# Two convolution blocks on one core: the 7x7 convolution's transfers split by partition halves between two queues, and the group norms' sums read out of their bank at once

## The chip, the cores and the metric

The kernel runs on one core of one Trainium2 chip. The metric is the device time of one execution in microseconds (us). A core has TensorE (PE in the profile, with PEld for the loading of its weights), VectorE (DVE), ScalarE (ACT), GpSimd (POOL) and SyncE (SP). Transfers are carried by 16 DMA engines. In this kernel SP and POOL each issue transfers on a queue of their own (q1 and q0 in the profile); ACT issues a few.

## The reference

The input x is (8, 96, 96, 192) in float32. Two blocks follow one another, each added to its input:

```python
# layer 0
x = x + L0(_gn(x))   # 192 -> 384 projection, 3x3 depthwise conv, four decaying scans,
                     # layer norm over channels, 384 -> 192 projection
# layer 1
x = x + L1(_gn(x))   # 7x7 depthwise conv, layer norm, 192 -> 768, gelu, 768 -> 192, scale

def _gn(v, G=32, eps=1e-5):
    g = v.reshape(B_, H_, W_, G, C_ // G)
    m = jnp.mean(g, axis=(1, 2, 4), keepdims=True)
    s = jnp.var(g, axis=(1, 2, 4), keepdims=True)
    return ((g - m) / jnp.sqrt(s + eps)).reshape(v.shape)
```

`_gn` is a group norm: the mean and the variance of 32 groups of 6 channels, for each of the 8 images. The 7x7 convolution works on every channel by itself.

## The kernel before

Five stages follow one another. The order of instructions on each engine is written out by hand (`tc.manual_schedule`): every engine works off its own list in program order.

- **A** (about 47 to 783 us of the span): for each image, 12 units. A unit turns a piece of the image with transposes (`turn`, L351, evicted with the group norm's scale and shift by ACT at L358 or DVE at L356), multiplies it by `win` (`project_full` L365, `project_rest` L378) and stores it. The transposes use a pool `pt` of two PSUM banks. While image b is projected, the statistics of image b+1 are gathered (`bn_stats` L320), and in units 9 to 11 the steps of its group norm are placed among the projection (`ends`, L468): `means` in unit 9, `squares` in 10, `powers` and `shift` later in 10, the spreading in 11.
- **B** (783 to 1846 us): the 3x3 convolution, as products with a band matrix, and the scans.
- **C** (1846 to 2930 us): 96 units of four blocks (`block_c`, transposes L833 and products L835), each finished one unit later by `finish_c` on DVE (`x1u`, L858, which empties the PSUM banks `po`, and `x1c`, L871). The group norm of the next layer, for a pair of images at a time, is gathered at L887, and its steps come one to a unit, each placed behind the unit's products and ahead of `finish_c`. It has a PSUM bank of its own (`gn_ps`).
- **D** (2930 to 3510 us): the 7x7 convolution. 16 steps of 12 channels (`conv_d`, L1030); the 12 are two sets of 6, called m = 2i and 2i+1. `load_d(m)` brings one set: six `xin` transfers (L753) and two `band` transfers (L758), of 64 partitions each; SP loads partitions 0 to 63 and GpSimd 64 to 127. Five sets fit, so set m waits until the convolution has done with set m-5. `scale_d` (DVE, L1015) applies the group norm to a set, one step ahead of its use. ACT evicts a step's outputs to `yo` (L1041; two buffers), with the first set's outputs in partitions 0 to 63 (k = 0) and the second set's in 64 to 127 (k = 1), and `store_d` (L1070) stores them to `Y_d`, all on GpSimd, k by turns. In the last step the first quarter of each row goes by SP (L1069) and the rest by GpSimd.
- **E** (3510 us to the end): the layer norm and the two big products. Its first load `y` (L1122) is on SP and reads the first quarter of the rows of `Y_d`.

The group norm's own steps are in `norm_steps` (L32). `means` sums the per-chunk means on DVE (L49), and two products with `avg` (L51, L52) put the group means into a PSUM bank; `squares` copies these out (`gm` L57, `mean` L59), sums the squares (L61 to L69) and multiplies them by `avg` (L71) into a second bank; `powers` reads that (`ve`, L75) and takes the power -0.5 on GpSimd; `shift` follows. Then `spread` brings scale and shift to all partitions (L332 in A; L903 and L911 in C).

In the profile the digits of a name are dropped: `X1_d`, `Y_d` and `Z2_d` stand there as `X_d`, `Y_d` and `Z_d`.

Of the kernel before, what the change touches and what calls it, by code (L numbers as in the profile page):

```python
# [8 lines left out]
F32 = mybir.dt.float32  # L9
AF = mybir.ActivationFunctionType  # L10
ALU = mybir.AluOpType
AX = mybir.AxisListType
# [3 lines left out]
GROUPS = 32  # L16
GN_EPS = 1e-5
# [14 lines left out]
def norm_steps(nc, pool, psum, tag, st, avg, count, neg_half):  # L32

    rows, n, k, _ = st.shape
    sub = 2 * k
    sv = st.rearrange("p n k (e t) -> p n (k e) t", t=3)  # L40
    rb = pool.tile([n, 2], F32, tag="gn_rb", name="gn_rb")
    t = {}

    def bank():
        return psum.tile([128, 512], F32, tag=tag, name="gn_ps")

    def means():
        ms = pool.tile([rows, n], F32, tag="gn_ms", name="gn_ms")
        nc.vector.tensor_reduce(ms, sv[:, :, :, 1], AX.X, ALU.add)  # L49
        t["ps"] = ps = bank()  # L50
        nc.tensor.matmul(ps[:, :n], avg, ms, start=True, stop=True)  # L51
        nc.tensor.matmul(ps[:n, n : n + 1], ms, avg[:, 0:1], start=True, stop=True)  # L52

    def squares():

        gm = pool.tile([rows, n], F32, tag="gn_gm", name="gn_gm")
        nc.vector.tensor_scalar(gm, t["ps"][:rows, :n], 1.0 / sub, None, ALU.mult)  # L57
        t["mean"] = mean = pool.tile([n, 1], F32, tag="gn_mean", name="gn_mean")
        nc.vector.tensor_scalar(mean, t["ps"][:n, n : n + 1], -1.0 / sub, None, ALU.mult)  # L59
        d = pool.tile([rows, n, sub], F32, tag="gn_d", name="gn_d", bufs=1)  # L60
        nc.vector.tensor_tensor(  # L61
            d, sv[:, :, :, 1], gm.unsqueeze(2).to_broadcast([rows, n, sub]), ALU.subtract
        )
        nc.vector.tensor_tensor(d, d, d, ALU.mult)
        nc.vector.scalar_tensor_tensor(
            d, sv[:, :, :, 2], 1.0 / count, d, ALU.mult, ALU.add
        )
        ds = pool.tile([rows, n], F32, tag="gn_ds", name="gn_ds")
        nc.vector.tensor_reduce(ds, d, AX.X, ALU.add)  # L69
        t["ps"] = ps = bank()  # L70
        nc.tensor.matmul(ps[:n, 0:1], ds, avg[:, 0:1], start=True, stop=True)  # L71
# [12 lines left out]
@with_exitstack  # L84
def conv_blocks_kernel(
# [31 lines left out]
    nc = tc.nc  # L117
    B, S, _, D = x.shape
# [8 lines left out]
    GS = D // GROUPS  # L127

    const = ctx.enter_context(tc.tile_pool(name="const", bufs=1))
# [9 lines left out]
    BP = B // 2  # L139
    PH = 3  # L140
# [18 lines left out]
    HB = 21  # L159
# [12 lines left out]
    ones = const.tile([64, 128], F32, name="ones")  # L172
    nc.vector.memset(ones, 1.0)


# [47 lines left out]
    with ExitStack() as ph:  # L223
# [14 lines left out]
            nc.scalar.dma_start(bin_, b_in.rearrange("(m p) -> p m", p=128))  # L238


        member = cp.tile([GROUPS, 2, GROUPS, GS], F32, name="member")
        for i in range(2):
            nc.vector.tensor_copy(
                member[:, i],
                ident[:GROUPS, :GROUPS].unsqueeze(2).to_broadcast([GROUPS, GROUPS, GS]),
            )
        memberf = member.rearrange("p i g s -> p (i g s)")

# [222 lines left out]
        with tc.manual_schedule():  # L471
# [13 lines left out]
            for b in range(B):  # L485
                more = b + 1 < B
                for t in range(n_t):
# [28 lines left out]
                    k, j = divmod(t, NJ)  # L516
# [250 lines left out]
    with ExitStack() as ph:  # L767
# [108 lines left out]
        def group_steps(x1c, k, i):  # L876


            bp, part = divmod(k, NH)
            n = part * NS + i  # L880
            if n == 0:
                gn[0] = sp.tile([S, 2 * GROUPS, NH * NS, 6], F32, tag="gn_st", name="gn_st", bufs=1)
            st = gn[0]
            w = slice(i * WC // NS, (i + 1) * WC // NS)

            def step(b, g):
                nc.vector.bn_stats(  # L887
                    st[:, b * GROUPS + g, n], x1c[:, g * GS : (g + 1) * GS, w, b]
                )

            bn = [lambda b=b, g=g: step(b, g) for g in range(GROUPS) for b in range(2)]
            per = -(-len(bn) // (n_s - 1))
            steps = [bn[j : j + per] for j in range(0, len(bn), per)]
            if n < NH * NS - 1:
                return steps
            last, rb = norm_steps(nc, sp, ps_s, "gn_ps", st, avg, GS * WC // NS // 2, neg_half)
            held = []

            def spread():

                dg = sp.tile([2 * GROUPS, 2, 2 * GROUPS], F32, tag="gn_dg", name="gn_dg", bufs=1)
                for a in range(2):
                    nc.vector.tensor_scalar(  # L903
                        dg[:, a],
                        ident[: 2 * GROUPS, : 2 * GROUPS],
                        rb[:, a : a + 1],
                        None,
                        ALU.mult,
                    )
                ps = ps_s.tile([128, 512], F32, tag="gn_ps", name="ps_s1")  # L910
                nc.tensor.matmul(  # L911
                    ps[:, : 4 * GROUPS],
                    ones[: 2 * GROUPS],
                    dg.rearrange("p a g -> p (a g)"),
                    start=True,
                    stop=True,
                )
# [79 lines left out]
    with ExitStack() as ph:  # L997
# [12 lines left out]
        def scale_d(m, xin):  # L1010
            xv = xin.rearrange("q t a c (v b) -> q t a c v b", b=2)
            for b in range(B):
                sc, sh = (s1[:, a, b % 2, b // 2, m : m + 1] for a in range(2))
                xw = xv[:, :, b // 2, :, :, b % 2]
                nc.vector.tensor_scalar(xw, xw, sc, sh, ALU.mult, ALU.add)  # L1015
# [30 lines left out]
                        scale=1.0,  # L1046
                    )

        def store_d(yo, i):
            for bl in range(NB):  # L1050

                pieces = [(3, HB - 3)]
                if bl == 0:
                    pieces.append((HB - 3, HB))
                if bl == NB - 1:
                    pieces.append((0, 3))
                for k in range(2):
                    c = i * CD + k * HC
                    for lo, hi in pieces:
                        r = (S - HB - bl * HG) * PH  # L1060
                        src = yo[k * 64 + lo * PH : k * 64 + hi * PH, bl]
                        dst = Y_d[r + lo * PH : r + hi * PH, c // HC].rearrange(
                            "r b a c n -> r (b a c n)"
                        )
                        src = src.rearrange("r a c n -> r (a c n)")

                        n = NV * HC * 2 * WQ if i == D // CD - 1 else 0
                        if n:
                            nc.sync.dma_start(dst[:, :n], src[:, :n])  # L1069
                        nc.gpsimd.dma_start(dst[:, n:], src[:, n:])  # L1070
# [265 lines left out]
```

## Time and profile before

| | |
|---|---|
| median of 10 runs | 5964.9 us (5962.51 to 5969.27) |
| the profiled execution | 5969.09 us |
| its span, first to last instruction | 5967.3 us |
| mean granted TensorE clock | 0.974 |
| busy: PE, PEld, DVE, ACT, POOL | 95%, 66%, 58%, 41%, 44% of the span |
| q0 (GpSimd), q1 (SP) | 450.64 MB in 24.0%, 593.38 MB in 38.5% of the 16 engines' span |

A line of the timeline has the start in us, the time it took in us, the engine, the line of the kernel and the operation, what it writes and reads, how many instructions are merged, and in brackets how long the engine had been idle before and what released it. "SPq" and "POOLq" are the issuing side of a queue. A line of a windows table has the window, its length, the busy time and number of instructions of PE, PEld, DVE, ACT and POOL, the granted clock, the mean busy share of the 16 DMA engines, and GB/s. A line of the DMA view by queue has the packets, the MB and the time they took as a share of the window.

### The profile page before, as it was taken

What the parts mean: (1) busy time and instruction counts of PE and PEld (TensorE: products, weight loads), DVE (VectorE), ACT (ScalarE), POOL (GpSimd) and SP (SyncE); (2) the same over time, 40 slices, a digit from 0 to 9 for tenths busy, and PEclk for the clock granted to TensorE, in tenths of its full rate; (3) what the DMA queues carried; (4) which work ended last, traced back from release to release, by engine and by line L of the source; (5) the groups of instructions that cost most, each with busy time, mean ns of one, the idle gap of its engine ahead of it and who ended that gap; (6) DMA issues with size and microseconds to landing.
All of it is one profiled execution on the core that took longest, in us unless ns stands there. A gap on an engine that the chain in (4) does not pass through costs nothing.

```text
span 5967.3 us, 122712 instructions
## 1 busy us (share of the span) xinstructions
PE 5647.7 (95%) x48550; PEld 3956.8 (66%) x48550; DVE 3452.5 (58%) x8023; ACT 2429.5 (41%) x6146; POOL 2613.4 (44%) x2835
## 2 busy tenths in 40 slices
PE   6999989999998999999687769999999999999999
PEld 3655633333336989898666647777777777777777
DVE  5555469999995667777623234444444444444443
ACT  2444457777775555555343322222222222222222
POOL 1111148888886666666433323333333333333332
PEclk9999989999999999999888879999999999999999
DMA  7999779999987888888899953232323232323221
GB/s 203 284 282 262 219 208 245 246 244 244 244 236 202 263 262 265 263 267 261 240 292 289 289 154 79 64 80 64 80 62 77 64 80 63 79 64 80 64 64 39
DMA packets 634143, 1054.48 MB, mean 177 GB/s; under 512 B 108976, under 2 KB 508929, under 8 KB 633569
## 3 DMA queue, kind: packets, MB, share of 16 engines
q1 hardware_dynamic: 510192, 593.38, 38.5%
q0 software_dynamic: 117248, 450.64, 24.0%
q8 instruction: 384, 6.29, 0.5%
q10 hardware_dynamic: 6128, 2.61, 0.2%
q14 instruction: 191, 1.56, 0.1%
HBM read 585.19 MB, written 476.72 MB: 178 GB/s over the span
## 4 chain that ended last, share of the span: by engine, by line
PE 78%; DMA 6%; DVE 1%; issue 1%; POOL 1%; SPq 0%; ACT 0%; POOLq 0%; DVEq 0%; ACTq 0%
PE po L1225 19%; PE po L835 14%; PE hp L1195 12%; PE pl L582 10%; PE hp L1205 7%; PE pa L603 5%; PE pt L833 4%; PE py L1030 3%; DMA Y_d<-yo 3%; PE pa L606 2%; DMA xin<-X_d 2%; PE pt L1178 2%; DVE xin L1015 1%; DMA X_d<-x1c 0%; SPq L1069 0%
## 5 line engine op out<-in xcount | busy, mean ns | idle before, releaser
L1214 ACT ACTIVATE g<-hp,b0g 128x384 f32<-128x384 f32 x1152 | 563.3, 587 | 1834.5 <-PE hp L1205 1834.5
L1225 PE MATMUL po<-w1g,g 128*128 128x192 f32 x6912 | 1162.7, 327 | 0.0
L1225 PEld LDWEIGHTS po<-w1g,g 128*128 128x128 f32 x6912 | 1121.7, 190 | 1.1 <-issue 1.1
L835 PE MATMUL po<-wc,mt 128*96 128x193 f32 x4608 | 913.0, 333 | 0.0
L1182 DVE COPY yT<-pt 128x384 f32<-128x384 f32 x288 | 248.5, 863 | 1044.0 <-PE pt L1178 1043.6
L1195 PE MATMUL hp<-yT,w0w 128*128 128x384 f32 x2304 | 782.4, 490 | 0.4 <-DVE yT L1182 0.4
L835 PEld LDWEIGHTS po<-wc,mt 128*96 128x96 f32 x4608 | 701.8, 163 | 68.6 <-ACT mean L839 65.1
L1243 POOL DMA_DIRECT2D out_dram<-xo x576 | 340.3, 593 | 880.8 <-DVE xo L1232 847.3
L582 PE MATMUL pl<-pin,band 34*32 34x380 f32 (+1 forms) x13824 | 629.1, 489 | 18.6 <-DMA pin<-P_d 18.6
L1195 PEld LDWEIGHTS hp<-yT,w0w 128*128 128x128 f32 x2304 | 429.8, 191 | 257.9 <-issue 4.3
L612 DVE TENSOR_TENSOR_SCAN z<-decay,loc 128x768 f32<-128x768 f32 x288 | 505.9, 1756 | 59.6 <-ACT loc L591 30.3
L652 POOL TENSOR_TENSOR mo<-mo,z 128x768 f32<-128x768 f32 x288 | 529.4, 1839 | 3.4 <-ACT mo L607 0.4
L1030 PE MATMUL py<-xin,band 63*64 63x248 f32 (+1 forms) x6912 | 400.4, 391 | 133.7 <-DVE xin L1015 133.7
L29 POOL TENSOR_TENSOR rs<-rs_ve,neg_half 96x8 f32<-96x8 f32 x96 | 159.1, 1657 | 830.1 <-DVE rs_ve L28 830.1
L621 DVE TENSOR_TENSOR_SCAN z<-decay,z 128x768 f32<-128x768 f32 x288 | 498.2, 1730 | 0.0
L582 PEld LDWEIGHTS pl<-pin,band 34*32 34x32 f32 x13824 | 232.9, 107 | 396.9 <-issue 395.7
L1030 PEld LDWEIGHTS py<-xin,band 63*64 63x64 f32 x6912 | 334.4, 141 | 199.3 <-DVE xin L1015 125.3
L842 ACT ACTIVATE sq<-pt,mean 96x384 f32<-96x384 f32 x768 | 442.9, 577 | 25.7 <-ACT mean L839 0.8
L603 PE MATMUL pa<-loc,mix 128*32 128x384 f32 x3456 | 431.9, 493 | 0.0
L606 PE MATMUL pa<-last,down 96*32 96x384 f32 x1152 | 426.8, 493 | 0.9 <-ACT mo L607 0.9
L1205 PE MATMUL hp<-yT,w0w 64*128 64x384 f32 x2304 | 423.5, 500 | 0.0
L365 PE MATMUL pm<-xT,win 128*128 128x384 f32 x1152 | 397.3, 495 | 5.0 <-DVE po L389 5.0
(116 smaller groups left out, 7682.9 us busy)
## 6 DMA issues: line engine op xcount, KB each, us to landing
P_d<-po POOLq DMA_DIRECT2D x96, 1152.0 KB, 9.7
pin<-P_d SPq DMA_DIRECT2D x192, 576.0 KB
mt<-M_d SPq DMA_DIRECT2D x576, 192.0 KB
xq<-in_x_dram SPq DMA_DIRECT2D x96, 576.0 KB
xr<-in_x_dram SPq DMA_DIRECT2D x384, 144.0 KB
X_d<-x1u POOLq DMA_DIRECT2D x192, 288.0 KB, 4.1
X_d<-x1c SPq DMA_DIRECT2D x192, 288.0 KB
y<-Y_d SPq DMA_DIRECT2D x24, 2304.0 KB
```

What stands on the lines that cost most here:

```text
L582: nc.tensor.matmul(pls[g][at * RB : (at + 1) * RB, :, lo:hi], band[rows, c, kh, :], pin[rows, c, :, NJ - 1 - j, lo + kh - 1 : hi + kh - 1] ...
L603: nc.tensor.matmul(pa[at], mix[:, i, at], loc[:, q], start=True, stop=True)
L606: nc.tensor.matmul(pa[at], down[:, to], last[:, q], start=True, stop=True)
L612: nc.vector.tensor_tensor_scan(zf, decay_f, loc.rearrange("p q n -> p (q n)"), 0.0, ALU.mult, ALU.add)
L621: nc.vector.tensor_tensor_scan(zr, decay_f, zr, 0.0, ALU.mult, ALU.add)
L652: nc.gpsimd.tensor_tensor(m, m, z, ALU.add)
L835: nc.tensor.matmul(po[:S, b], lhs[m], wc[:, m], start=(m == 0), stop=(m == NC - 1))
L1030: nc.tensor.matmul(pys[t // 2][g][k * 64 : (k + 1) * 64, t % 2, :, lo:hi], pair[k][0][rows, c, d * ZS : d * ZS + 64], pair[k][1][rows, t, ...
L1195: nc.tensor.matmul(hps[m, q], w0w[:, 2 * q, m * 128 : (m + 1) * 128], yT[:, 2 * q], start=True, stop=False,)
L1205: nc.tensor.matmul(hps[m, q], w0w[p, 1, m * 128 : (m + 1) * 128], yT[p, 1], start=False, stop=True,)
L1214: nc.scalar.activation(g[:, m, q], hps[m, q], AF.Gelu, bias=b0g[:, m : m + 1], scale=1.0)
L1225: nc.tensor.matmul(po[:, q], g[:, m, q, k * 128 : (k + 1) * 128], w1g[:, m], start=(m == 0), stop=(m == NE - 1),)
```

## The change

There are two independent parts.

In **D**, `store_d` is called for one half k at a time: k = 0 on SP, k = 1 on GpSimd, so each queue loads and stores partitions of one half only. The stores of step i-1 move into step i: SP issues its stores ahead of its loads of the step, GpSimd its stores behind its loads. In the last step every row goes in four pieces of a quarter each, the first quarters of all rows ahead of the others, on both queues.

In the **group norms**, `means` and `squares` copy the sums out of PSUM right behind the products that made them, instead of in the next step. The operands `ms`, `ds`, `member`, `dg`, `ones` and the results are filled up to 128 rows or columns, two of them by a memset.

```diff
     def means():
-        ms = pool.tile([rows, n], F32, tag="gn_ms", name="gn_ms")
-        nc.vector.tensor_reduce(ms, sv[:, :, :, 1], AX.X, ALU.add)
-        t["ps"] = ps = bank()
-        nc.tensor.matmul(ps[:, :n], avg, ms, start=True, stop=True)
-        nc.tensor.matmul(ps[:n, n : n + 1], ms, avg[:, 0:1], start=True, stop=True)
+        ms = pool.tile([rows, 128], F32, tag="gn_ms", name="gn_ms")
+        nc.vector.memset(ms[:, n:], 0.0)
+        nc.vector.tensor_reduce(ms[:, :n], sv[:, :, :, 1], AX.X, ALU.add)
+        ps = bank()
+        nc.tensor.matmul(ps[:, :n], avg, ms[:, :n], start=True, stop=True)
+        nc.tensor.matmul(ps[:, n : n + 1], ms, avg[:, 0:1], start=True, stop=True)
+
+        t["gm"] = gm = pool.tile([rows, n], F32, tag="gn_gm", name="gn_gm")
+        nc.vector.tensor_scalar(gm, ps[:rows, :n], 1.0 / sub, None, ALU.mult)
+        t["mean"] = mean = pool.tile([128, 1], F32, tag="gn_mean", name="gn_mean")
+        nc.vector.tensor_scalar(mean, ps[:, n : n + 1], -1.0 / sub, None, ALU.mult)
 
     def squares():
 
-        gm = pool.tile([rows, n], F32, tag="gn_gm", name="gn_gm")
-        nc.vector.tensor_scalar(gm, t["ps"][:rows, :n], 1.0 / sub, None, ALU.mult)
-        t["mean"] = mean = pool.tile([n, 1], F32, tag="gn_mean", name="gn_mean")
-        nc.vector.tensor_scalar(mean, t["ps"][:n, n : n + 1], -1.0 / sub, None, ALU.mult)
+        gm = t["gm"]
...
-        ds = pool.tile([rows, n], F32, tag="gn_ds", name="gn_ds")
-        nc.vector.tensor_reduce(ds, d, AX.X, ALU.add)
-        t["ps"] = ps = bank()
-        nc.tensor.matmul(ps[:n, 0:1], ds, avg[:, 0:1], start=True, stop=True)
+        ds = pool.tile([rows, 128], F32, tag="gn_ds", name="gn_ds")
+        nc.vector.memset(ds[:, n:], 0.0)
+        nc.vector.tensor_reduce(ds[:, :n], d, AX.X, ALU.add)
+        ps = bank()
+        nc.tensor.matmul(ps[:, 0:1], ds, avg[:, 0:1], start=True, stop=True)
+        t["ve"] = ve = pool.tile([128, 1], F32, tag="gn_ve", name="gn_ve")
+        nc.vector.tensor_scalar(ve, ps[:, 0:1], 1.0 / sub, GN_EPS, ALU.mult, ALU.add)
 
     def powers():
-        ve = pool.tile([n, 1], F32, tag="gn_ve", name="gn_ve")
-        nc.vector.tensor_scalar(ve, t["ps"][:n, 0:1], 1.0 / sub, GN_EPS, ALU.mult, ALU.add)
-        nc.gpsimd.tensor_tensor(rb[:, 0:1], ve, neg_half[:n, 0:1], ALU.pow)
+        nc.gpsimd.tensor_tensor(rb[:, 0:1], t["ve"], neg_half[:, 0:1], ALU.pow)
...
-        def store_d(yo, i):
-            for bl in range(NB):
-
-                pieces = [(3, HB - 3)]
...
-                for k in range(2):
-                    c = i * CD + k * HC
+        def store_d(yo, i, k):
+
+            eng = (nc.sync, nc.gpsimd)[k]
+
+            w = BP * NV * HC * 2 * WQ
+            n = NV * HC * 2 * WQ if i == D // CD - 1 else w
+            for at in range(0, w, n):
+                for bl in range(NB):
+
+                    pieces = [(3, HB - 3)]
...
                     for lo, hi in pieces:
                         r = (S - HB - bl * HG) * PH
                         src = yo[k * 64 + lo * PH : k * 64 + hi * PH, bl]
-                        dst = Y_d[r + lo * PH : r + hi * PH, c // HC].rearrange(
-                            "r b a c n -> r (b a c n)"
+                        dst = Y_d[r + lo * PH : r + hi * PH, 2 * i + k]
+                        eng.dma_start(
+                            dst.rearrange("r b a c n -> r (b a c n)")[:, at : at + n],
+                            src.rearrange("r a c n -> r (a c n)")[:, at : at + n],
                         )
-                        src = src.rearrange("r a c n -> r (a c n)")
-
-                        n = NV * HC * 2 * WQ if i == D // CD - 1 else 0
-                        if n:
-                            nc.sync.dma_start(dst[:, :n], src[:, :n])
-                        nc.gpsimd.dma_start(dst[:, n:], src[:, n:])
...
+            done = None
             for i in range(n_i):
                 pair, loads = loads[:2], loads[2:]
+
+                if done is not None:
+                    store_d(done, i - 1, 0)
                 for m in (2 * i + 3, 2 * i + 4):
                     if m < 2 * n_i:
                         loads.append(load_d(m))
+                if done is not None:
+                    store_d(done, i - 1, 1)
                 if i + 1 < n_i:
                     for k in range(2):
                         scale_d(2 * i + 2 + k, loads[k][1])
-                yo = op.tile([128, NB, BP * NV, HC, 2 * WQ], F32, tag="yo", name=f"yo_{i}")
+                done = op.tile([128, NB, BP * NV, HC, 2 * WQ], F32, tag="yo", name=f"yo_{i}")
                 for c in range(HC):
-                    conv_d(pair, c, yo, i)
-                store_d(yo, i)
+                    conv_d(pair, c, done, i)
+            for k in range(2):
+                store_d(done, n_i - 1, k)
```

More of the change, by code (lines that the diff above doesn't have):

```diff
@@ L40, in norm_steps @@
     sv = st.rearrange("p n k (e t) -> p n (k e) t", t=3)
-    rb = pool.tile([n, 2], F32, tag="gn_rb", name="gn_rb")
+    rb = pool.tile([128, 2], F32, tag="gn_rb", name="gn_rb")
     t = {}
@@ L171, in conv_blocks_kernel @@
     nc.vector.memset(neg_half, -0.5)
-    ones = const.tile([64, 128], F32, name="ones")
+    ones = const.tile([128, 128], F32, name="ones")
     nc.vector.memset(ones, 1.0)
@@ L238, in conv_blocks_kernel @@
             nc.scalar.dma_start(bin_, b_in.rearrange("(m p) -> p m", p=128))
-        member = cp.tile([GROUPS, 2, GROUPS, GS], F32, name="member")
+        member = cp.tile([128, 2, GROUPS, GS], F32, name="member")
         for i in range(2):
@@ L244, in conv_blocks_kernel @@
                 member[:, i],
-                ident[:GROUPS, :GROUPS].unsqueeze(2).to_broadcast([GROUPS, GROUPS, GS]),
+                ident[:, :GROUPS].unsqueeze(2).to_broadcast([128, GROUPS, GS]),
             )
@@ L899, in spread @@
             def spread():
-                dg = sp.tile([2 * GROUPS, 2, 2 * GROUPS], F32, tag="gn_dg", name="gn_dg", bufs=1)
+                dg = sp.tile([128, 2, 2 * GROUPS], F32, tag="gn_dg", name="gn_dg", bufs=1)
                 for a in range(2):
@@ L904, in spread @@
                         dg[:, a],
-                        ident[: 2 * GROUPS, : 2 * GROUPS],
+                        ident[:, : 2 * GROUPS],
                         rb[:, a : a + 1],
@@ L912, in spread @@
                     ps[:, : 4 * GROUPS],
-                    ones[: 2 * GROUPS],
+                    ones,
                     dg.rearrange("p a g -> p (a g)"),
@@ L1047, in conv_d @@
                     )
-        def store_d(yo, i):
-            for bl in range(NB):
-                pieces = [(3, HB - 3)]
[L1053 to L1056, printed above, removed]
-                for k in range(2):
-                    c = i * CD + k * HC
+        def store_d(yo, i, k):
[5 more added lines that the diff above has]
+                    pieces = [(3, HB - 3)]
+                    if bl == 0:
+                        pieces.append((HB - 3, HB))
+                    if bl == NB - 1:
+                        pieces.append((0, 3))
                     for lo, hi in pieces:
```

## The prediction

> **What bounds the kernel now.** I read the page's slices first, then the stages by windows, then the stage that the larger half of the diff edits, then the waits and the order of time at the places that the smaller half edits.
>
> ```profile
> PE   6999989999998999999687769999999999999999
> ...
> DMA  7999779999987888888899953232323232323221
> ```
>
> A slice is 149 us. PE is at 8 or 9 tenths almost everywhere; counted from 1, the exceptions are slice 1 and slices 20 to 24. In 21 to 23, and there alone, DMA is full while PE is not. The stage windows (us, then busy PE, PEld, DVE, ACT, POOL, granted clock, DMA share, GB/s) say the same of A (per-image projection), C (group norm between the layers) and D (the 7x7 convolution):
>
> ```profile
> 47.00:783.00 736.00, 711.73 (x3538) 430.66 (x3536) 381.87 (x1310) 313.53 (x577) 112.04 (x134) 0.99 0.84 246
> ...
> 1846.00:2930.00 1084.00, 1076.13 (x6936) 973.77 (x6936) 752.64 (x2657) 632.32 (x2304) 722.56 (x578) 1.00 0.87 258
> 2930.00:3510.00 580.00, 408.68 (x6944) 341.99 (x6944) 174.38 (x341) 201.35 (x384) 206.99 (x386) 0.83 0.94 274
> ```
>
> A and C are PE's (97% and 99%); D is DMA's (94%, PE 70%). So in D a change is worth what it does to the transfers, in A and C what it does to PE's few gaps.
>
> Inside D, one steady step (ten of them are the last row: 332.3 us, 33.2 us each, DMA share 0.99) is made of stretches with very different rates:
>
> ```profile
> 2977.00:3005.00 28.00, 23.79 (x401) 23.15 (x405) 13.63 (x24) 10.44 (x20) 2.83 (x5) 0.83 1.02 279
> 3133.00:3139.00 6.00, 0.11 (x4) 0.00 (x0) 3.20 (x6) 0.93 (x3) 2.02 (x4) 0.80 1.02 208
> 3144.00:3155.00 11.00, 11.00 (x216) 9.49 (x212) 5.01 (x8) 6.26 (x12) 5.02 (x8) 1.00 1.01 350
> 3156.00:3159.00 3.00, 3.00 (x64) 2.59 (x60) 0.00 (x0) 2.10 (x4) 1.38 (x3) 1.00 0.98 393
> 3107.40:3439.70 332.30, 251.94 (x4320) 211.24 (x4320) 96.17 (x160) 125.89 (x240) 129.17 (x240) 0.86 0.99 289
> ```
>
> The share is 1 in all of them; the rate is not. The DMA view by queue tells them apart. In 3144 to 3155 SP's queue loads (51%) while Pool's stores (48%): 350 GB/s. In 3156 to 3159 Pool stores nearly alone: 393. In 2977 to 3005 both queues load, one half of the partitions each: 279. From 3133 Pool's loads run alone, into partitions 64 to 127 only, and the engines count as full at 208:
>
> ```profile
> q0 software_dynamic: 221, 1.04, 102.9%
> ```
>
> That last stretch is the waste of a step. It comes from the order on the queues:
>
> ```profile
> 3132.74 1.73 SPq L753 DMA_DIRECT2D xin<-X_d  x3
> 3132.80 0.53 POOL L1070 DMA_DIRECT2D Y_d<-yo  x1 [1.86 <-ACT yo L1041]
> ...
> 3158.64 1.03 POOL L753 DMA_DIRECT2D xin<-X_d  x2 [0.66 <-DMA Y_d<-yo]
> ...
> 3168.57 4.74 DVE L1015 TENSOR_SCALAR xin<-xin,s 128x576 f32<-128x576 f32 x8 [19.20 <-DMA xin<-X_d]
> ```
>
> When a convolution ends (3132.5) SP issues its half of the next loads; Pool first issues all 16 stores and reaches its own loads 26 us later. DVE's scaling, which releases PE, waits for that half.
>
> **D, the steady step.** A step moves 12 xin transfers of 384 KB, 4 bands of 312 KB, 12 stores of 270 KB and 4 of 54 KB (issue view): 6.00 MB in, 3.54 MB out, 9.54 MB (289 GB/s by 33.2 us is 9.6). Before: SP 3.0 MB, Pool 6.5 MB. After: 4.77 MB on each; SP stores 1.77 MB and then loads 3.0, Pool loads 3.0 and then stores 1.77. No instruction is added but for the last step. If the queues share the engines evenly, a step has three stretches: SP's stores beside 1.77 MB of Pool's loads; the other 1.23 MB of Pool's loads beside as much of SP's; the rest of SP's loads beside Pool's stores. The first and third mix a store queue with a load queue, as 3144 to 3155 did: 2 x 3.54 MB at 350 GB/s is 20.2 us. The middle has both halves loading, as 2977 to 3005: 2.46 MB at 279 is 8.8 us. Sum 29.0 us against 33.2: 4.2 us a step. The first two convolutions run on loads issued before any store, and the last needs none, so 13 steps (2 to 14) gain: **-55 us**. The mixed rate is the unknown: in the row the stores took both halves by turns, now one half. Its bounds are 279 (a one-half store hurts a load as another load does) and 393 (stores alone). I take 350, the only row with a store queue beside a one-half load queue.
>
> What comes next if transfers get faster is the loop over two steps. From the end of convolution i-1: ACT's last eviction about 1 us, SP's stores 10.1, SP's half of load 2i+3 (1.50 MB: 1.23 in the middle stretch, 0.27 at 175 GB/s) 10.3, landing about 2, scaling 4.75, convolution 25: 53 us, 26.6 a step. That floor gives 6.6 x 13 = -86. The stores that now stand ahead of SP's loads are in this loop, and so cost nothing until the step is under 26.6. Pool's stores, now behind its loads, must be done before ACT writes the same yo two convolutions later: about 2 us after the 29.0, and ACT's first write comes about 5 us into a convolution; PSUM holds one more channel (3.8 us). Covered.
>
> **D's end.** The last stores become 32 pieces of 1536 B rows on each queue, and SP must issue all 32 before the first y load, against 16. Before, SP's 16 took 15.66 us from 3492.22 and y was issued at 3510.08. SP's waits show a transfer waiting for earlier ones of its queue; its first three came 0.36 us apart. Bounds: 32 x 0.36 = 11.5 us (y 4 us earlier) and 32 x 0.98 = 31 us (15 later). But the 0.98 was beside Pool's 4608 B rows, and the bytes are unchanged: 3.54 MB at 393 is 9 us. I take **+1**.
>
> **Group norm in A** (7 of 8 images; the first is exposed and pays two memsets, some 0.3 us). Before, the bank with the means waits for `squares` one unit later:
>
> ```profile
> 134.92 0.55 PE L351 MATMUL pt<-ident,xq 96*128 96x96 f32 x4
> 136.28 0.55 PE L351 MATMUL pt<-ident,xq 96*128 96x96 f32 x4 [0.81 <-ACT xT L358]
> ...
> 140.15 0.18 DVE L57 TENSOR_SCALAR gn_gm<-gn_ps 96x32 f32<-96x32 f32 x1
> ```
>
> so the transposes have one bank and PE waits 0.81 us, twice an image (136.28 and, for the squares, 144.79). DVE is idle there, reads at once about 135.3, and the bank is free when the second transpose wants it. 7 x 2 x 0.81 = **-11 us**. The filled operands (128 instead of 32 columns, 0.16 against 0.11 us a matmul by L51 and L52) cost under 1 us in all.
>
> **Group norm in C** (3 of 4; behind the last one lie 6.2 us of PE L712 and a load that lands at 2976, which hide it). Here reading at once is a new wait:
>
> ```profile
> 2162.87 1.18 DVE L49 TENSOR_REDUCE gn_ms<-gn_st 96x64 f32<-96x768 f32 x1
> 2164.18 1.39 DVE L858 SCALAR_TENSOR_TENSOR x1u<-po,rs,xr 96x192 f32<-96x192 f32 x4
> ...
> 2167.53 0.28 PE L52 MATMUL gn_ps<-avg,gn_ms 96*64 96x1 f32 x2
> ...
> 2174.62 0.28 PE L71 MATMUL gn_ps<-avg,gn_ds 96*64 96x1 f32 x2 [1.12 <-DVE gn_ds L69]
> ```
>
> PE reaches the norm's matmul only after its unit, at 2167.3. DVE, done reducing at 2164.1, must now wait there for `gm`; queued behind it are x1u and x1c of the unit before (2.6 us), whose banks PE needs, and then the squares (5.8 us), for which PE already waits. gm and mean end about 2168.2, x1u and x1c 2170.9; the chain that began at 2168.36 begins 2.5 us later (and is 0.1 us shorter, gm and mean against a memset), and a second wait, for `gn_ve`, holds x1u again: 0.7. Bounds: 0 (DVE makes it up) and 3.7 (the whole shift). I take 3.1: 3 x 3.1 = **+9 us**.
>
> **Sum**: -55 + 1 - 11 + 9 = -56. Profiled execution: 5969.1 (span 5967.3 and 1.8 around it) - 56 = 5913; it lies 4.2 above the median, so the median is 5964.9 - 56 = **5909**.
>
> **Rivals.**
> 1. The queues pass one after the other, so that overlap gives nothing and a step stays at 33.2: -1 us, **5964**. For it: SP issued six loads from 3132.74, and q0 alone moved until 3138. Against: 279 GB/s with two loading halves against 208 with one, a third more. The Trainium skill's SBUF — State Buffer, section "Can I just issue two DMAs to hit both halves?", has this rule: two such transfers, measured, gain 6% and serialize. This trace disagrees (279 against 208). By the page's 6% the middle stretch would take 2.4 us more, and the sum would be -25. Chance 0.13.
> 2. Slower: a store that reads one half collides on it as loads do. Then a step with halves kept apart runs at 279 throughout: 9.6 / 0.279 = 34.4 us, 13 x 1.2 = +16, with -1 from the rest **5980**. It decides below 292 GB/s in the mixed stretches (7.08 MB in 24.2 us). For it: today's fast stores alternate halves. Against: the x1c stores from 96 partitions ran at 399 GB/s (2952 to 2961), two thirds of it, 266, out of one half, where loads stop at 208. Chance 0.12.
> 3. Mixed stretches near 393, the loop is next: 26.6 a step, -86 - 1 = **5878**. For it: single moments of 3144 to 3155 pass 400 GB/s in the DMA view. Against: 350 as the mean over 11 us. Chance 0.12.
>
> **Numbers.** The forecast (step 28 to 31 us, 5892 to 5932) has 0.63. A measurement can tell about 0.2%, 12 us. Faster: forecast and rival 3, 0.75; same: rival 1, 0.13; slower: rival 2, 0.12. The range must take in rivals 1 and 3 (with C's and the end's lower bounds, -86 - 11 + 3 = -94) and leaves out rival 2: 5870 to 5966.
>
> **What would show it.** Steps of 29 us in D, no stretch near 208 GB/s, q0 and q1 near half each; PE's 0.81 us before L351 gone in A; PE's wait before the squares' matmul in C at 3 us or more. D's step at 33 or more proves me wrong.

## The result and the profile after

| | before | after |
|---|---|---|
| median | 5965.0 us (29 runs) | 5921.2 us (8 runs, 5913.1 to 5935.2) |
| ratio | | 0.9928, 95% interval 0.9920 to 0.9937 |
| profiled execution (span) | 5969.1 (5967.3) | 5914.8 (5913.0) |

The profiled execution lost 54.3 us where 56 were forecast. The median lost 43.8: four of the eight runs lie at 5925 to 5935, the others at 5913 to 5917, which the experiments take up. The stages, each measured from the first or last product of its own line, add up to the 54.3 us:

| stage | forecast | measured |
|---|---|---|
| A, up to B's first product (792.4 to 775.8) | -11 | -16.5 |
| B | 0 | +0.5 |
| C, from B's last product to D's first (1151.1 to 1161.9) | +9 | +10.9 |
| D, first to last product (527.2 to 481.8) | -55 | -45.5 |
| D's last product to the end | +1 | -3.7 |

First the page's slices of the changed kernel, PE and DMA as before. Slices 21 to 23 still have DMA full; PE is at 7, 8, 8 there, where it was at 8, 7, 7, and at 8 for 6 in slice 20.

```profile
PE   6999989999998999999878869999999999999999
...
DMA  7999789999987889888899952232323232323221
```

Then the stages by windows (A, C, D; the columns are those of the first windows table):

```profile
40.00:766.50 726.50, 710.96 (x3554) 435.45 (x3554) 385.75 (x1335) 312.99 (x577) 112.71 (x135) 0.99 0.85 250
...
1829.50:2925.00 1095.50, 1080.04 (x6936) 977.65 (x6936) 752.57 (x2666) 632.27 (x2304) 724.21 (x578) 0.99 0.86 255
2925.00:3459.30 534.30, 417.61 (x6944) 358.37 (x6944) 173.32 (x341) 197.81 (x384) 149.78 (x282) 0.88 0.95 298
```

PE's share in D went from 70% to 78%, the rate from 274 to 298 GB/s. C now takes longer. D is still bound by its transfers, as the steady part says. The first row below is eleven steps (3 to 13): 329.5 us, 30.0 us each. The others are stretches inside it.

```profile
3053.30:3382.80 329.50, 283.57 (x4754) 239.47 (x4750) 107.45 (x181) 135.32 (x265) 92.91 (x174) 0.93 1.00 320
3117.50:3123.00 5.50, 5.50 (x112) 5.50 (x108) 3.49 (x6) 0.00 (x0) 2.35 (x5) 1.00 1.02 389
3063.00:3071.00 8.00, 8.00 (x159) 6.99 (x156) 1.97 (x4) 4.41 (x9) 2.24 (x4) 1.00 1.03 293
3204.00:3209.00 5.00, 3.80 (x64) 3.00 (x59) 4.39 (x8) 2.10 (x4) 1.09 (x2) 1.00 0.97 337
3369.00:3375.00 6.00, 6.00 (x120) 4.16 (x116) 0.00 (x0) 4.05 (x10) 1.03 (x2) 1.00 1.02 272
```

In 3117.5 to 3123 both queues store for the most part: 389. In 3063 to 3071 SP stores and Pool loads: 293. In 3204 to 3209 SP loads and Pool stores: 337. In 3369 to 3375 both load: 272.

For all eleven steps I gave every packet to a transfer by its place in its queue's order, and fitted the rate of each microsecond to what the two queues carried in it. This is an estimate, because the 16 engines work off one transfer at different times: the 64 packets of the `band` transfer that ends Pool's loads of one step start between 3103.3 and 3113.6. It gives:

| what the two queues carry | time in the eleven steps | GB/s |
|---|---|---|
| both load | 119 us | 286 |
| SP stores, Pool loads | 88 us | 314 |
| SP loads, Pool stores | 86 us | 340 |
| both store | 36 us | 397 |

A store beside a load (the two middle rows) goes at 327 GB/s, not at the 350 of the forecast, and there are stretches of two storing queues that it did not have. The split itself is even, by the DMA view of the queues in 3053 to 3383:

```profile
q0 software_dynamic: 11875, 52.12, 50.1%
q1 hardware_dynamic: 11463, 52.79, 49.3%
```

The order of time shows how two storing queues come about. SP's eight stores of a step begin at 3113.92. Pool's stores of the step before are only just issued (its last at 3115.24, each after a wait for an earlier transfer), so their data moves beside SP's. ACT then waits 10.28 us for the stores out of the yo that it has to write, and PE 1.98 for ACT:

```profile
3113.92 7.45 SPq L1073 DMA_DIRECT2D Y_d<-yo  x8
3115.24 0.51 POOL L1073 DMA_DIRECT2D Y_d<-yo  x1 [1.50 <-DMA band<-Z_d]
...
3117.28 1.03 POOL L759 DMA_DIRECT2D xin<-X_d  x2 [1.53 <-DMA xin<-X_d]
...
3122.82 4.69 SPq L759 DMA_DIRECT2D xin<-X_d  x3
...
3125.62 2.57 ACT L1047 ACTIVATE yo<-py,dwb 128x512 f32<-128x512 f32 x5 [10.28 <-DMA Y_d<-yo]
...
3126.36 2.13 PE L1036 MATMUL py<-xin,band 63*64 63x256 f32 x22 [1.98 <-ACT yo L1047]
```

The group norm in A, by the order of time. The transposes at L357 are one run of eight without the 0.81 us, and gm is read at 133.22, right behind its products:

```profile
132.82 0.36 PE L55 MATMUL gn_ps<-avg,gn_ms 96*128 96x1 f32 x2
133.05 1.10 PE L357 MATMUL pt<-ident,xq 96*128 96x96 f32 x8
133.22 0.19 DVE L58 TENSOR_SCALAR gn_gm<-gn_ps 96x32 f32<-96x32 f32 x1 [1.55 <-PE gn_ps L55]
```

In C, DVE now waits 3.74 us for the means with x1u queued behind, PE's next products wait 0.66 for x1u, the squares' product waits 1.95 where it had waited 1.12, and the products behind it wait 0.57 for x1u again:

```profile
2152.16 0.22 DVE L58 TENSOR_SCALAR gn_gm<-gn_ps 96x64 f32<-96x64 f32 x1 [3.74 <-PE gn_ps L55]
...
2152.37 1.38 DVE L864 SCALAR_TENSOR_TENSOR x1u<-po,rs,xr 96x192 f32<-96x192 f32 x4
...
2153.15 1.23 PE L841 MATMUL po<-wc,mt 128*96 128x193 f32 x6 [0.66 <-DVE x1u L864]
...
2160.58 0.38 PE L77 MATMUL gn_ps<-avg,gn_ds 96*128 96x1 f32 x2 [1.95 <-DVE gn_ds L75]
...
2161.90 2.25 PE L841 MATMUL po<-wc,mt 128*96 128x193 f32 x6 [0.57 <-DVE x1u L864]
```

Behind that last wait the granted clock is halved for 3.4 us (a windows row, the clock is 0.51 here). The same happens at each of these three norms, and at none of them before the change:

```profile
2161.80:2165.20 3.40, 3.30 (x11) 2.89 (x12) 2.11 (x7) 0.82 (x3) 2.34 (x3) 0.51 0.47 141
```

D's end: SP's 32 store issues took 13.72 us, where 16 had taken 15.66, and y is issued 13.7 us after the last product has begun, where it was 17.7:

```profile
3441.33 13.72 SPq L1073 DMA_DIRECT2D Y_d<-yo  x32
3455.43 0.33 SPq L1135 DMA_DIRECT2D y<-Y_d  x1
```

### The profile page after: what moved, and what is told of

The parts are those of the page before. It is cut to its first block, busy times and chain, and to the rows that moved or that the text cites. A ratio compares the mean times of both kernels' runs of the same rounds, so it can differ in the third digit from the quotient of the medians.

```text
span 5913.0 us, 122909 instructions
## 1 busy us (share of the span) xinstructions
PE 5652.1 (96%) x48550; PEld 3974.2 (67%) x48550; DVE 3452.2 (58%) x8047; ACT 2424.9 (41%) x6146; POOL 2557.1 (43%) x2731
## 4 chain that ended last, share of the span: by engine, by line
PE 77%; DMA 7%; issue 1%; DVE 1%; SPq 1%; POOL 0%; ACT 0%; ACTq 0%; POOLq 0%; DVEq 0%
PE po L1238 19%; PE po L841 14%; PE hp L1208 12%; PE pl L588 10%; PE hp L1218 7%; PE pa L609 5%; PE pt L839 4%; PE pa L612 2%; DMA xin<-X_d 2%; PE pt L1191 2%; DMA Y_d<-yo 2%; PE py L1036 2%; DMA band<-Z_d 2%; DMA X_d<-x1c 0%; SPq L1073 0%
## 5 line engine op out<-in xcount | busy, mean ns | idle before, releaser
L618 DVE TENSOR_TENSOR_SCAN z<-decay,loc 128x768 f32<-128x768 f32 x288 | 505.9, 1756 | 60.2 <-ACT loc L597 30.6
L1036 PEld LDWEIGHTS py<-xin,band 63*64 63x64 f32 x6912 | 350.5, 140 | 137.8 <-DVE xin L1021 38.6
```

Source lines behind the costliest of these rows:

```text
L618: nc.vector.tensor_tensor_scan(zf, decay_f, loc.rearrange("p q n -> p (q n)"), 0.0, ALU.mult, ALU.add)
L1036: nc.tensor.matmul(pys[t // 2][g][k * 64 : (k + 1) * 64, t % 2, :, lo:hi], pair[k][0][rows, c, d * ZS : d * ZS + 64], pair[k][1][rows, t, ...
```

## The experiments

Twelve kernels. Medians and ratios are against the kernel before on the same chip; D (first to last product) and the step (mean of steps 3 to 13) are of the profiled execution.

| kernel | median, us | ratio, 95% interval | D | step |
|---|---|---|---|---|
| the change | 5921.2 | 0.9928 (0.9920 to 0.9937) | 481.8 | 30.0 |
| D's part alone | 5916.2 | 0.9924 (0.9911 to 0.9937) | 475.9 | 30.1 |
| group norms alone | 5961.8 | 1.0003 (0.9994 to 1.0012) | 526.8 | 33.1 |
| C as before | 5905.9 | 0.9909 (0.9893 to 0.9924) | 474.2 | 29.7 |
| both queues store first | 5958.3 | 0.9987 (0.9975 to 0.9999) | 511.3 | 31.7 |
| roles exchanged | 5927.2 | 0.9931 (0.9909 to 0.9952) | 495.0 | 30.9 |
| stores of both halves by turns | 5902.3 | 0.9903 (0.9889 to 0.9917) | 466.0 | 28.9 |
| stores crossed over | 5914.4 | 0.9922 (0.9907 to 0.9936) | 480.9 | 30.0 |
| Pool's stores in the middle | 5933.7 | 0.9958 (0.9944 to 0.9973) | 492.7 | 30.7 |
| 54 filling products | 5920.7 | 0.9925 (0.9913 to 0.9937) | 475.7 | 29.7 |
| 54, and C as before | 5907.2 | 0.9902 (0.9887 to 0.9916) | 475.0 | 29.7 |
| 26, and C as before | 5911.6 | 0.9906 (0.9893 to 0.9920) | 470.6 | 29.1 |
| 40, C as before, halves by turns | 5882.4 | 0.9857 (0.9840 to 0.9873) | 462.5 | 28.9 |

### The two parts apart

D's part alone: `norm_steps` and its operands as before the change.

> Only the 7x7 convolution's part of the change; the group norms stay as before. Theory (the transfers in D gain, the group norms gain 17 us in A and give 10 back in C): D takes 29 to 30 us a step as in the changed kernel, A ends as before, C has no new wait; the profiled execution is 7 us above the changed kernel's 5914.8, about 5922, and some 47 us under the kernel before. Rival (the group norms carry a good part of the gain, or the parts help one another): 5940 or more.

The group norms alone: `store_d` and its calls as before the change.

> Only the group norms' part of the change; the 7x7 convolution stays as before. Theory: A is 17 us shorter (two waits of 0.8 us for a bank less, for each of 7 images, and a little more), C 10 us longer (DVE waits for PE's sums ahead of the work that frees PE's banks, 3.4 us at each of 3 norms), together 5958, 0.1% under the kernel before. Rival (reading at once is a gain in both stages): C no longer than before, 5948 or less. Rival (the wait in C eats all): 5965 or more.

D's part alone gives all of the gain: 0.9924 beside 0.9928. The group norms alone measure nothing, 1.0003. In their profile B begins 14 us earlier and C takes 10 us longer (the three units of C that hold a norm take 14.8, 13.3 and 11.3 us for 13.1, 11.3 and 11.7, at each of three norms): the two halves of that part nearly cancel. Their median, 5961.8, lies between the theory's 5958 and the second rival's 5965.

### The sums read late in C, early in A

```diff
         ps = bank()
         nc.tensor.matmul(ps[:, :n], avg, ms[:, :n], start=True, stop=True)
         nc.tensor.matmul(ps[:, n : n + 1], ms, avg[:, 0:1], start=True, stop=True)
+        t["ps"] = ps
+        if not late:      # late=True in C: called in squares() and powers()
+            take_means()
```

> The changed kernel, but in stage C the sums are read in the next step of the norm, as before the change; in A they are read at once, and the operands stay filled to 128. Theory (in C reading at once only adds DVE's wait): C's three norms cost 2.8 us each as in the kernel before instead of 6.2, so 10 us less than the changed kernel: profiled execution about 5905. Rival (C became longer by the wider operands): C stays 10 us longer, about 5915.

Median 5905.9, with the three units of a norm at 13.2, 11.3 and 11.3 us and the granted clock at 1 behind each norm. C takes 1149.6 us from B's last product to D's first, as before the change (1151.1), against 1161.9. So reading at once costs C 12 us: the forecast's sign and, roughly, its size are shown. The wider operands are still there, so they are not the cause.

Its runs spread from 5891.8 to 5926.4, and its profile (5921.4) is a high one. The windows of B's start say why. PE is busy, but the granted clock stays at 0.50 until past 840:

```profile
783.60:800.00 16.40, 13.26 (x168) 5.20 (x176) 5.78 (x4) 4.78 (x12) 0.49 (x2) 0.50 0.84 170
800.00:820.00 20.00, 20.00 (x198) 5.15 (x190) 12.95 (x8) 7.98 (x19) 5.54 (x7) 0.50 0.78 174
820.00:840.00 20.00, 20.00 (x200) 5.10 (x192) 10.07 (x7) 7.76 (x18) 6.11 (x7) 0.50 0.31 67
840.00:860.00 20.00, 20.00 (x280) 5.95 (x272) 12.28 (x9) 10.00 (x24) 10.77 (x13) 0.72 0.62 144
```

In the profile of the change it is back at 803. B is 21 us longer here, with the same instructions.

### Which queue begins with what

Both queues begin a step with their stores:

```diff
                 if done is not None:
                     store_d(done, i - 1, 0)
+                    store_d(done, i - 1, 1)
```

> The changed kernel, but GpSimd too issues its half of the stores ahead of its loads. Theory (a store queue beside a load queue runs at 350 GB/s, two load queues at 279, two store queues at 390, and the mixture makes the step): 3.54 MB at 390 and 6.0 MB at 279 are 30.6 us a step, against 29.9 in the changed kernel, 13 x 0.7 = 9 us slower than it, about 5924; the wait of ACT for yo's stores, and PE's behind it, is gone. Rival (that wait sets the step in the changed kernel): steps of 28 us or less, 5890. Rival (the order between loads and stores is what gains, not the even split): steps back at 33 us, 5958.

The roles exchanged, SyncE loading first and GpSimd storing first (the 0 and 1 of the two calls change places):

> The change with the two queues' roles exchanged in D: SyncE loads its half first and then stores k = 0, GpSimd stores k = 1 first and then loads. Theory (what counts is that one queue begins a step with stores and the other with loads, so that the two kinds are spread in time): by symmetry the same as the change, D 476 to 486 us, steps of 30 us, 5921 us. Rival (it matters which queue begins with the stores: GpSimd issues one transfer at a time behind the waits for its eight last, as in the kernel before, where its loads came 26 us after a convolution's end; now its 8 stores stand ahead instead of 16): its half of the loads is late, steps of 31.5 to 33 us, D 500 to 520, 5940 to 5960 us.

Bytes and split are the change's in both. With stores first on both queues the step is 31.7 us, between the theory's 30.6 and the 33 of the third rival, and D is 511.3: of the 45 us that the change gained in D, 29.5 are gone. The median, 5958.3, is the third rival's figure, but not by its step alone: the profile also has B's longer start, 21 us, and the runs spread from 5937 to 5975. In the exchanged kernel D is 495, between the theory and the lower edge of its rival; its median and interval (0.9909 to 0.9952) do not tell it from the change. Its profile too has B's longer start, so only D's length is read from the two. Their DMA share is 0.99 to 1.00: the engines are never idle and merely slower, 307 GB/s with stores first:

```profile
3084.80:3433.50 348.70, 284.79 (x4758) 239.87 (x4756) 108.00 (x181) 138.27 (x264) 96.36 (x176) 0.89 1.00 307
```

So the even split alone is not the gain; the order is a large part of it. By the same estimate as above, with stores first both queues load at 279 GB/s for 215 us of the eleven steps and both store at 363 for 89, and a store stands beside a load, at 331, for only 43 us; the change has 119, 36 and 174 us of these. The mixture differs far more than the rates. In the exchanged kernel it lies between (both load for 171 us).

### Does ACT's wait for Pool's stores cost anything

```diff
                 for m in (2 * i + 3, 2 * i + 4):
                     if m < 2 * n_i:
                         loads.append(load_d(m))
-                if done is not None:
-                    store_d(done, i - 1, 1)
+                    if done is not None and m == 2 * i + 3:
+                        store_d(done, i - 1, 1)
```

> The change with GpSimd's stores of k = 1 moved between its loads of the first and of the second set of a step (after the change they come behind both). Theory (ScalarE's wait for those stores before it may write the same yo, 62 us in eleven steps, holds TensorE for some 2 us a step, which the prediction had called covered): the wait goes, steps of 27.5 to 29 us, D 455 to 470, 5897 to 5910 us. Rival (the transfers alone set the step, at 320 GB/s and a DMA share of 1.00): steps of 30 us as in the change, only with the wait elsewhere, 5921 us. Second rival (loads of the second set come late behind the stores, as when both queues begin with stores, which gave steps of 31.7 us): D 500 to 511, 5940 to 5950 us.

The waits of this kernel's steady steps (engine, line, what it waited for: us in total, times, longest):

```profile
DVE xin L1021 <- DMA xin<-X_d: 136.8, 13, 15.9
...
ACT yo L1047 <- DMA Y_d<-yo: 8.3, 1, 8.3
```

The wait is gone (8.3 us, where the same view of the change has 62.0 in six), and the step is 30.7, no shorter. PE now waits for DVE's scaling, which waits for loads. So that wait was there, against the prediction's "covered", but taking it away gained nothing; the DMA share is 1.00 with it and without it. What the wait costs by itself is not shown, because the edit also brings the loads of the second set later. The theory falls; the second rival has it half (D 493, forecast 500 to 511).

### The halves

One queue, both halves by turns:

```diff
-        def store_d(yo, i, k):
-            eng = (nc.sync, nc.gpsimd)[k]
+        def store_d(yo, i, part):
+            eng = (nc.sync, nc.gpsimd)[part]
...
+                for bl in range(part * 3, part * 3 + 3):
...
+                    for k in range(2):
```

> The change, but each queue stores both halves of half the rows (bl 0 to 2 on SyncE, 3 to 5 on GpSimd, the two halves by turns) instead of one half of all rows. Bytes, order on the queues and the last step are the change's. Theory (what gains is the even split and the order; a store reads one half as fast as two by turns): the same as the change, steps of 30 us, D 474 to 484, 5915 to 5925 us. Rival (the halves count: a store out of both halves disturbs the other queue's loads less, as the 350 GB/s of the kernel before in 3144 to 3155): steps of 29 us or less, D 460 to 470, 5900 to 5910 us. Second rival (the halves count the other way, a queue is best kept to its own half): steps of 31 us or more, D 490 and up, 5930 and up.

The stores crossed over, each queue storing the half that the other one loads (`eng = (nc.gpsimd, nc.sync)[k]`, and the 0 and 1 of the two calls exchanged):

> The change with the stores crossed over: SyncE, which loads partitions 0 to 63, stores partitions 64 to 127 (k = 1), and GpSimd, which loads 64 to 127, stores 0 to 63. So where one queue stores beside the other's loads, both now work on the same half. Order, bytes and rows are the change's. Theory (a store that reads a half does not collide with a load that fills it, so halves count for loads alone): the same as the change, steps of 30 us, D 474 to 484, 5915 to 5925 us. Rival (the second rival of the prediction: a store out of a half collides with loads into it): the mixed stretches fall towards the 208 GB/s of one half alone, steps of 32 us or more, D 505 and up, 5945 us and up.

The windows of the kernel that stores by turns, its eleven steps and one stretch of each mixture (3064 to 3070 SP stores and Pool loads, 3109 to 3115 SP loads and Pool stores):

```profile
3057.70:3375.50 317.80, 276.39 (x4756) 240.49 (x4751) 106.53 (x180) 135.40 (x265) 93.75 (x176) 0.93 1.00 333
3064.00:3070.00 6.00, 6.00 (x120) 6.00 (x116) 2.96 (x6) 3.95 (x9) 2.15 (x4) 1.00 1.03 352
3109.00:3115.00 6.00, 5.10 (x94) 3.24 (x86) 4.77 (x8) 3.86 (x8) 1.64 (x3) 1.00 0.95 350
```

These stretches have 352 and 350 where the change's had 293 and 337. Over whole profiles the difference is smaller and less clear. By the estimate over eleven steps a store beside a load goes at 349 GB/s here and at 346 in the last kernel below; it goes at 327 in the change and at 329 to 348 in the five other profiles with its D. The step is 28.9 us and D 466, as the first rival expected; the six profiles with the change's D have steps of 29.1 to 30.1 and D of 471 to 482. So the gain by turns is some 10 us, of which chance may hold a part: the best of the six comes within 5 us. The last kernel below repeats it. In the crossed kernel both transfers of a mixed stretch use the same half, and the step is the change's:

```profile
3056.40:3386.70 330.30, 282.16 (x4754) 241.60 (x4750) 108.52 (x182) 135.41 (x265) 92.78 (x175) 0.93 1.00 320
```

The estimate for a store beside a load is 328 GB/s here. So it makes no difference whether the store beside a load shares its half, and the prediction's rival 2 (a collision on the half, under 292 GB/s in the mixed stretches) is refuted. The two kernels with stores by turns have the shortest D of all; that stores out of one half are slower beside loads is likely, and what in the chip would make them so no run here shows.

### B's start

Products that nothing uses, ahead of B's first (54 of them):

```diff
+            busy = ps_a.tile([128, GB * S], F32, tag="pa", name="pa")
+            for _ in range(54):
+                nc.tensor.matmul(
+                    busy, mix[:, 0], zero.rearrange("p b h -> p (b h)"), start=True, stop=True
+                )
```

> The change, and 54 products of the kernel's `mix` with zeros (384 columns each, into an unused bank) put ahead of stage B's first product, so that TensorE is busy while the first `pin` loads are under way. Nothing of the result uses them. Theory (the granted clock of 0.5 at B's start follows from TensorE's idle 12.5 and 6.3 us there, and the further 21 us of some executions from the same low clock lasting to 845 us): B's first units take 10.5 us instead of 18.6 and 15.1, or 12.7 us less, and no execution has the 21 us more: 5900 to 5908 us, and a spread under 10 us. Rival (the clock falls for another reason, as the change of work from stage to stage): units of 18.6 and 15.1 as in the change, 5921 us with the same spread. Second rival (the products run on into the time when `pin` has landed, and cost what they gain): 5915 to 5925 us with units of 10.5.

> Both additions: the group norm of C reads the sums one step later, as before the change, and TensorE is kept busy at B's start. Theory (C's reading at once costs 10 us and the low clock 13 to 34 us, each on its own): 5885 to 5898 us, D 474 to 482, C's norms 13.2, 11.3, 11.3. Rival (the lower median of the kernel that only read later in C, 5906 us, was itself a matter of how B's start fell): no better than that, 5900 to 5910 us.

The clock is at 1 when B begins and its units take 10.5 us from the start. That part of the theory is shown: with the idle time filled the low clock does not come. But I had sized a product by the 0.34 us of a row of A, which is one record, and each product leaves two (108 in the trace, 35.1 us, 0.65 us a product): 54 last until 801.8 and cost what they gain, the second rival. The rest of the theory falls: the runs still spread from 5905 to 5934 at equal mean clocks (0.981 to 0.982), so B's start is not all of the spread. With C as before it is 5907, the rival's figure.

> Both additions with the number of filling products put right: the group norm of C reads the sums one step later, as before the change, and 26 products (not 54, which took 0.65 us each and held B's first product until 801.8) keep TensorE busy at B's start, some 17 us from 766.8. Theory (the filling products end as `pin` lands, and the clock is at 1 when B begins): B begins at 784 with units of 10.5, 18 us earlier than with 54 products, and so 5885 to 5893 us, the best of all. Rival (the gap left after the products, a few us until the second set of `pin` lands, is enough to lower the clock again): units of 18 and 15 us at B's start, 5900 us or more.

With 26 the profile is 5891.9, as the theory had it, but the median 5911.6. In that profile B begins at 783.8, PE then waits twice for pin (1.00 and 2.03 us), and after the second the clock falls again, to a mean of 0.64 for 4.7 us:

```profile
785.60:792.10 6.50, 6.44 (x144) 3.21 (x144) 3.19 (x2) 3.55 (x9) 0.25 (x1) 1.00 1.01 220
794.10:798.80 4.70, 4.69 (x58) 1.61 (x62) 4.15 (x3) 1.78 (x5) 0.24 (x1) 0.64 0.98 185
```

The other four runs have mean clocks of 0.978 to 0.981, this one 0.984; that B's long low clock came back in them is likely, and not shown.

> The three additions together: each queue stores both halves of half the rows, C's group norm reads the sums one step later, and 40 filling products at B's start (40 by 0.65 us is 26 us, from 766.8 to 793, when the second set of `pin` is nearly there). Theory (the three are independent: C 10.9 us less than the change, D 466, B ending at about 1797 in every execution): 1797 and 1150 for C puts D's first product at 2947, D 466, the rest 2471, 1.8 around the span: 5886 us, 5880 to 5892. Rival (stage D's length varies by some 10 us from one kernel to the next for reasons that are not in its code, 471 to 482 us with the change's own D, and 466 was such a lucky fall): D back at 470 to 482, 5890 to 5902 us.

5882.4 us, 0.9857 of the time before, with runs from 5881.1 to 5883.5: the best kernel, and within the theory's range (D 462.5, and B's last product at 1798.6 for 1797). D is 12.5 and 8.1 us shorter than in the two kernels that have the change's D with C as before and 54 or 26 products (475.0 and 470.6), so the gain by turns has come twice. Here the fill ends at 793.1 and the clock never drops:

```profile
767.00:793.00 26.00, 25.88 (x80) 15.12 (x80) 0.00 (x0) 0.06 (x1) 2.44 (x3) 1.00 0.86 263
793.00:820.00 27.00, 27.00 (x529) 11.01 (x528) 23.59 (x15) 18.48 (x45) 9.08 (x12) 1.00 0.86 178
```

## Why the prediction was right, and where its steps were off

- **Direction, bound and place: right.** D was DMA's, and the share stayed at 1 while the rate rose from 289 to 320 GB/s.
- **D's step: mechanism right, one term mis-sized.** "2 x 3.54 MB at 350 GB/s" was the term. The 350 came from stores that took both halves by turns; the text named that difference and still took it. One-half stores beside loads went at 327 by the estimate, and in the two kernels that store by turns at 349 and 346. With 327 the sum would be 21.7 + 8.8 = 30.5 us; the measured 30.0 is a little lower, as part of the stores runs beside stores, at 397. 42 us of the 45.5 are 13 steps of 3.2.
- **The three stretches: there, but with a fourth.** By the estimate a store stands beside a load for 15.8 us of a step (the forecast had 20.2), both queues load for 10.8 (8.8), and both store for 3.3, which the forecast did not have: Pool's stores wait behind its loads, each for an earlier transfer, and reach into the next step beside SP's.
- **"Covered": wrong as a claim, harmless as far as the runs show.** ACT waited for these stores, 62 us in six waits; the kernel without that wait was no faster.
- **D's end, +1: the figure was -3.7, and most of it is not D's end.** The 32 issues cost 0.43 us each, near the lower bound of 0.36, so y was issued 4.0 us earlier and the nearer row was the one not taken. But E's first big product came only 1.0 us earlier after D's last (43.8 us for 44.8). The rest lies in E, whose code is the same and which took 2425.9 to 2430.5 us from that product on in the fourteen profiles; this part is scatter.
- **A, -11: it was -16.5.** Each image's three norm units went from 25.2 to 23.1 us, and 7 x 2.1 is 15: the two waits of 0.81 and half a microsecond more. The rest is in the first image, where a wait of PE for DVE was 3.6 us instead of 5.0; with the group norms alone it was 5.0 again, and B began 14.3 us earlier, not 16.5.
- **C, +9: it was +10.9, near the forecast in part by luck.** The mechanism was there: DVE held at gm, x1u late, and the squares' product later still. But it is worth 2.1 us a norm (0.66 and 0.57 for x1u, 0.83 more ahead of the squares' product), where 3.1 were forecast, and the sign named for it, a wait of 3 us or more ahead of that product, did not come (1.95). The sum had put the clock at nothing: 3.4 us at half the clock behind each norm cost some 1.7 us, about half of C's 10.9 for three norms; the unit after is 0.4 us shorter than before. With the sums read late the clock stays at 1 and C is as before.
- **Rival 1: refuted** by steps of 30.0. The Trainium skill's SBUF — State Buffer ("Can I just issue two DMAs to hit both halves?", 6%) disagrees with this trace again: both queues loading moved 272 GB/s in the row above and 286 by the estimate, one half alone 208 before. **Rival 3** needed 393 in the mixed stretches; no kernel's mean over both mixtures passed 349.
- **What the sum left out:** the clock, behind C's norms and at B's start. That the errors of the terms (A and the end lower, D and C higher) nearly cancelled in the profile, -54 for -56, is luck. The median is 12 us above the forecast, as part of the runs lose something more; that B's low clock, 21 us longer in some profiles, is one such loss is likely, and not shown for these runs.

## What to carry to other kernels

A rate read from a stretch is shown only for the access pattern of that stretch: if the change alters the pattern (here, stores out of one half and no longer by turns), measure the rate before building a sum on it, or keep the pattern. A DMA share of 1 is not a rate: what runs beside what moved it here from some 280 GB/s (two loads) to some 390 (two stores). Two queues with the same bytes are not yet balanced: at an equal split and full engines the order of loads and stores alone moved a step from 30.0 to 31.7 us. Idle time of TensorE can cost more than its length, at B's start and behind C's waits of 2 us, so look at the granted clock behind every new wait and where the next stage begins.

## What was not expected of the hardware

- Stores that alternate between the halves of the partitions ran beside loads at 346 and 349 GB/s, stores out of one half at 327 to 348 (estimates over eleven steps); whether the load fills the same half changed nothing (328, steps of 30.0).
- After 12.5 and 6.3 us of idle the granted clock stayed at 0.50 through 19.7 us of unbroken work in the change (783.6 to 803.3), and for over 60 us of mostly unbroken work in another execution of nearly the same code. The Trainium skill's TensorE: Matmul & The Clock Gate (section "Part 1: The HAM clock gate (the "warmup" mystery)") lets full speed return after some 3.4 us of sustained work; these rows do not agree. The same section's rule against idle gaps of more than some 3.4 us was not enough either: gaps of 1.00 and 2.03 us, 6.4 us apart, came before a fall to 0.64, and in C a gap of 1.95 us, with one of 0.57 behind it, before a fall to 0.51.
- Filling TensorE's idle time ahead of B with 40 or 54 unused products kept the clock at 1.
